# Where span attention's steps stand in the first stretch of a half batch: ahead of the second product with the values, or behind it

## The chip, the cores and the metric

The kernel runs on one core of a Trainium2 chip. The metric is the device time of one execution in microseconds (us), the median of three runs. All data are 32-bit floats. The engines of the core are PE (matrix products), DVE (vector operations), ACT (activations and copies), POOL (a second, slower engine for elementwise work) and SP (which issues transfers). Each runs its own instructions in order; they wait for each other by semaphores.

## What is computed

One layer of a perceiver: cross attention of 64 positions per batch element over a context of 1601 keys, then span attention over the 64 positions, then a feed-forward part with a shared expert and eight routed ones. Each part has a layer norm in front and a residual around it. There are 32 batch elements, a model width of 256 and 16 heads of 16.

```python
def reference(x, ctx_1024, mask_1x1xSxS2_bf1, ...):
    def _L0_xattn_ref(q, k, v, mask, ...):
        qh = _split_heads(q @ wq_w.T + wq_b)
        kh = _split_heads(k @ wk_w.T + wk_b)
        vh = _split_heads(v @ wv_w.T + wv_b)
        scores = jnp.einsum('bhqd,bhkd->bhqk', qh, kh) / jnp.sqrt(jnp.float32(D_K))
        scores = jnp.where(mask, scores, jnp.float32(-1000000000.0))
        attn = jax.nn.softmax(scores, axis=-1)
        out = jnp.einsum('bhqk,bhkd->bhqd', attn, vh)
        ...
        return out @ wo_w.T + wo_b
    def _L0_attn_ref(h, W_span, W_val, W_out):
        ...
        mean = jax.nn.sigmoid(span[..., 0]) * m
        soft = jax.nn.softplus(span[..., 1])
        diff = pos[None, None, :] - mean[..., None]
        scores = -soft[..., None] * (diff * diff)
        attn = jax.nn.softmax(scores, axis=-1)
        out = jnp.matmul(attn, value)
        ...
        return out @ W_out.T
    ...
    x = x + _L0_xattn_ref(_layernorm(x, axis=-1), ctx_1024, ctx_1024, mask_1x1xSxS2_bf1, ...)
    x = x + _L0_attn_ref(_layernorm(x, axis=-1), ...)
    x = x + _L0_ffn_ref(_layernorm(x, axis=-1), ...)
    return x
```

## The kernel before

**Tiling.** Cross attention goes by half batches: one batch element and 8 of its 16 heads. There are 64 of them, numbered n (b = n // 2, c = n % 2). The keys are cut into 13 blocks of 124, in four groups of 4, 3, 3 and 3 blocks. Scores are held transposed (keys on the partitions, four pairs of heads j = 0 to 3 beside each other). Two batch elements make a tile of 128 rows for the query projection, span attention and the feed-forward part: 16 tiles.

**The loop.** The main loop (L680) is a pipeline over half batches. In iteration n it computes the scores of half batch n + 1, the softmax of n, and the products of n - 1 with the values. It has four stretches, g = 0 to 3, one for each group of keys, which are counted through as 4n + g. PE, DVE, ACT and POOL execute their instructions in just the order in which the program issues them: the scheduler is held to it by `manual_schedule` (L648). So the order in the source is the order on each engine.

One iteration does this:

- Ahead of g = 0: `values(n-1, 0)` (L545), the first product with the values, 52 small products (104 matmul instructions, as each takes two) on PE, and the exponentials of the last pair of n - 1 on ACT.
- g = 0: `scores(n+1, 0)` (PE; DVE adds the mask to each of the four banks, L486), during which `turned_maxima(n)` transposes the maxima on PE (pm, L514) and DVE reduces them (mc, L521). Then one group of keys of the next batch element (pk, L442), and `maxima_along_rows` (L525), which spreads the maxima over the partitions on PE (pb, L529) and copies them on ACT (mb, L533). Then, for n above 0, `values(n-1, 1)`, the second product. If c = 0, that completes a batch element: `finish_steps(b-1)` (L620) is begun, its first piece copies the sums on ACT (o, L625), and the rest is put on the agenda of stretch 4n + 1 (L709). Then `less_maxima(n, 0)` (L536, POOL, 3.7 us each), `run(4n)`, and `first_maxima(n+1)` (L498), a copy on ACT with which the running maxima of the next half batch start.
- g = 1, 2, 3: `scores(n+1, g)` with the running maxima on DVE (L507) between the additions, keys (pk), values of the next batch element (pv, L458), `less_maxima(n, g)`, `run(4n+g)` and the exponentials of pair g - 1.

All of these products but the sums of the values and the running maxima take their PSUM bank from one pool of six.

**The agenda.** The short steps of the other parts are spread over the stretches. `agenda[s]` is a list of generators; `run(s)` (L614) takes the list in the order in which it was filled and advances each generator to its next `yield`, whose value says how many stretches later it goes on: it is then appended to that later stretch's list. Three kinds of generators use it:

- `span_steps(t)` (L214), 16 steps for a tile. It starts two stretches after the first of a half batch with n = 0 mod 4.
- `query_steps` (L402), the queries of the next tile, from the second stretch of n = 1 mod 4.
- `finish_steps` (L620): the sums' reciprocals (pr on PE, L628; rin on DVE, L632), and the product oT (DVE, L635), from which a tile's `span_steps` start one stretch later.

Since the period of a tile is four half batches, it is fixed what the first stretch of each holds:

| n mod 4 | steps in stretch 4n (`run(4n)`) |
|---|---|
| 0 | the span product po2 (16 products on PE, L327) and its copy o2T (ACT, L333) |
| 1 | two transposes tr_h (PE, L203) and the copy hT (ACT, L225) |
| 2 | the small operations on mean and slope (DVE, L273 to L289), which use part of the bank of the running maxima; the query product pq (PE, L412) and four copies qbd (ACT, L420) |
| 3 | one exponential (ACT, L305) |

In the stretch behind it, 4n + 1, stand for n = 0 mod 4 the rest of `finish_steps` and the span step po3 (PE, L337), x (DVE, L340), its statistics (DVE, L181 to L187), the power rstd_f (POOL, L189) and the transfer x_kept (SP, L342). For n = 2 mod 4 there are the rest of `finish_steps`, a span step on POOL (L294) and the last query step (POOL, L427).

The last half batch and the feed-forward part follow the loop and are not touched.

Of the kernel before, what the change touches and what calls it, by code (L numbers as in the profile page):

```python
# [76 lines left out]
def perceiver_kernel(ctx: ExitStack, tc: tile.TileContext, a: dict[str, bass.AP], out: bass.AP):  # L77
    nc = tc.nc
# [15 lines left out]
    def mm_bank(name: str):  # L94
        return ps_mm.tile([P, 512], F32, tag="mm", name=name)
# [277 lines left out]
    def pair_of(n: int, j: int):  # L373
        return prob[:CHUNK, place(n, j // 2), j % 2]
# [25 lines left out]
    def query_steps(t: int):  # L400
        spread = spread_of(xs[t], f"q{t}")
        yield 1  # L402
        xn = normalised(xs[t], spread, f"q{t}")
        yield 1
        ps = transposed(xn, f"q{t}")
        xnT = work.tile([P, 2, P], F32, tag="xnT", name=f"xnT_{t}")
        nc.vector.tensor_copy(xnT, ps)
        yield 1
        pq = mm_bank(f"pq_{t}")
        for c in range(2):  # L410
            for i in range(2):
                nc.tensor.matmul(  # L412
                    pq[:, c * P : (c + 1) * P], lhsT=wqT[:, i, c * P : (c + 1) * P],
                    rhs=xnT[:, i, :], start=(i == 0), stop=(i == 1),
                )

        q = work.tile([P, 2, 2, 2, S], F32, tag="qbd", name=f"qbd_{t}")
        for c in range(2):
            for e in range(2):
                nc.scalar.activation(  # L420
                    q[:, c, :, e, :], pq[:, c * P : (c + 1) * P].rearrange("p (b q) -> p b q", b=2),
                    AF.Identity, bias=bq4[:, c, e : e + 1], scale=own4[:, e : e + 1],
                )
        qbd[t] = q
        yield 1

        nc.gpsimd.tensor_tensor(xs[t], xs[t], bo_row, ALU.add)  # L427

    def load_context(b: int):
        for g in range(len(GROUPS)):  # L430
            load_piece(b, g)
        if b % 2 == 0 and b // 2 + 1 < NTILE:
            t = b // 2 + 1
            load_x(t)
# [34 lines left out]
    def scores(n: int, g: int, between=(), then=None):  # L469

        b, c = halves[n]
        c0, nb = GROUPS[g]
        pss = [mm_bank(f"psc_{b}_{c}_{g}_{j}") for j in range(4)]
        for k in range(nb):
            for j, ps in enumerate(pss):
                at = (c0 + k) * CHUNK
                nc.tensor.matmul(  # L477
                    ps[:CHUNK, k * P : (k + 1) * P],
                    lhsT=kTs[c][32 * j : 32 * j + 32, at : at + CHUNK],
                    rhs=qbd[b // 2][32 * j : 32 * j + 32, c, b % 2, :, :],  # L480
                    start=True, stop=True, tile_position=(32 * j, 0),
                )
        between = deque(between)
        held = then() if then else None
        for j, ps in enumerate(pss):
            nc.vector.tensor_tensor(  # L486
                pair_of(n, j)[:, c0 : c0 + nb, :].rearrange("p k (e q) -> p k e q", e=2),
                ps[:CHUNK, : nb * P].rearrange("p (k e q) -> p k e q", k=nb, e=2),
                madd[:CHUNK, c0 : c0 + nb, None, :].to_broadcast([CHUNK, nb, 2, S]), ALU.add,
            )  # L490
            if between:
                maximum(n, between.popleft())
            if j == 1 and held is not None:
                maxima_of_rows(*held)
# [3 lines left out]
    def first_maxima(n: int):  # L498
        nc.scalar.copy(mrun[:CHUNK].rearrange("p (r i) q -> p r i q", r=2), block_of(n, 0))  # L499

    def maximum(n: int, k: int):

        dst = mrun
        if k == NKC - 1:
            dst = mxs[n] = work.tile([P, 4, P], F32, tag="mx", bufs=1, name="mx")
        dst, run = (m[:CHUNK].rearrange("p (r i) q -> p r i q", r=2) for m in (dst, mrun))
        nc.vector.tensor_tensor(dst, block_of(n, k), run, ALU.max)  # L507

    def turned_maxima(n: int):

        m = mxs.pop(n)
        ps = mm_bank("pm")
        for j in range(4):
            nc.tensor.transpose(  # L514
                ps[:, j * CHUNK : (j + 1) * CHUNK], m[:CHUNK, j, :], ident[:CHUNK, :CHUNK]
            )
        return ps, work.tile([P, 4], F32, tag="mc", name="mc")
# [7 lines left out]
    def maxima_along_rows(col):  # L525

        ps = mm_bank("pb")
        for j in range(4):
            nc.tensor.transpose(  # L529
                ps[:CHUNK, j * P : (j + 1) * P], col[:, j : j + 1].to_broadcast([P, CHUNK]), ident  # L530
            )
        m = work.tile([P, 4, P], F32, tag="mb", bufs=1, name="mb")
        nc.scalar.copy(m[:CHUNK].rearrange("p j q -> p (j q)"), ps[:CHUNK])  # L533
        return m

    def less_maxima(n: int, j: int, m, engine):  # L536
        sj = pair_of(n, j)
        engine.tensor_tensor(  # L538
            sj, sj, m[:CHUNK, j, None, :].to_broadcast([CHUNK, NKC, P]), ALU.subtract
        )  # L540

    def exponentials(n: int, j: int):
        nc.scalar.activation(pair_of(n, j), pair_of(n, j), AF.Exp)  # L543

    def values(n: int, r: int):  # L545

        b, c = halves[n]
        v = vs[b % 2]
        for k in range(NKC):
            kn = min(CHUNK, KEYS - k * CHUNK)  # L550
            for j in range(4):
                h = 4 * r + j
                nc.tensor.matmul(  # L553
                    pvs[32 * j : 32 * j + DK + 1, c, r, :],
                    lhsT=v[:kn, k, 8 * c + h, :],
                    rhs=pair_of(n, h // 2)[:kn, k, (h % 2) * S : (h % 2) * S + S],
                    start=(k == 0), stop=(k == NKC - 1), tile_position=(0, 32 * j),
                )
# [29 lines left out]
    def linear_factor(u: int):  # L588
        quarter, hc = divmod(u, NHC)
        nc.scalar.activation(  # L590
            gated_at(quarter, hc), half_unit(u, sw3), AF.Identity, bias=b3twice[:, hc : hc + 1]
        )
        linear.add(u)
# [20 lines left out]
    def run(stretch: int):  # L614
        for steps in agenda.pop(stretch, []):
            wait = next(steps, None)
            if wait:
                agenda[stretch + wait].append(steps)
# [61 lines left out]
    for n, (b, c) in enumerate(halves[:-1]):  # L680
        if c == 0 and b + 1 < B:
            load_context(b + 1)
        if c and b % 2 == 0 and b // 2 + 1 < NTILE:
            agenda[4 * n + 1].append(query_steps(b // 2 + 1))

        def project(f, *args):
            if b + 1 < B:
                f(b + 1, *args)

        if n:  # L690
            values(n - 1, 0)
            exponentials(n - 1, 3)
        for g in range(len(GROUPS)):
            if g == 0:
                turned = []

                def turn():
                    turned.extend(turned_maxima(n))
                    return turned

                scores(n + 1, g, BETWEEN[g], turn)
                project(project_keys, c, 0)
                m = maxima_along_rows(turned[1])
                if n:
                    values(n - 1, 1)
                    if c == 0:
                        finish = finish_steps(b - 1, 4 * n + 1)
                        next(finish)
                        agenda[4 * n + 1].append(finish)  # L709
            else:  # L710
                scores(n + 1, g, BETWEEN[g])
                project(project_keys, c, g)
                if g == 1:
                    project(project_values, 3 * c)
                elif g == 2 and c:
                    project(project_values, 4)
                elif g == 3:
                    for u in range(5 if c else 1, 7 if c else 3):
                        project(project_values, u)
            less_maxima(n, g, m, nc.gpsimd)  # L720
            run(4 * n + g)
            for u in extra.get(4 * n + g, ()):
                linear_factor(u)
            if g == 0:
                first_maxima(n + 1)
            else:
                exponentials(n, g - 1)
        for k in BETWEEN[-1]:
            maximum(n + 1, k)
# [7 lines left out]
    m = maxima_along_rows(turned[1])  # L737
# [171 lines left out]
```

## Time and profile before

| | |
|---|---|
| median of 3 runs | 1637.11 us (1636.99 to 1639.4) |
| the profiled execution | 1636.38 us, its span 1634.6 us |
| granted clock of PE | 0.998 |
| four half batches (from one spreading of maxima to the fourth after it, 792.40 to 883.97) | 91.57 us |
| first product with the values to the scores behind it (n = 3 mod 4) | 1.58 us |
| POOL, one `less_maxima` | 3.73 us, 252 of them |

The profile is of one execution. Times count from the start of its span. A product's line in the timeline gives the start of its first matmul and the end of its last; since matmuls are pipelined, the distance between the starts of two groups tells how long the first holds the engine. PEld is the loading of the stationary operand, which overlaps the matmuls. A note in square brackets is the engine's idle time ahead of the instruction and what ended it. The chain of waits follows the work that ended last back in time, at each step to what released it, or to the instruction before it on its engine; an engine that is not on it has room.

### The profile page before, as it was taken

What the parts mean: (1) busy time and instruction counts of PE and PEld (TensorE: products, weight loads), DVE (VectorE), ACT (ScalarE), POOL (GpSimd) and SP (SyncE); (2) the same over time, 40 slices, a digit from 0 to 9 for tenths busy, and PEclk for the clock granted to TensorE, in tenths of its full rate; (3) what the DMA queues carried; (4) which work ended last, traced back from release to release, by engine and by line L of the source; (5) the groups of instructions that cost most, each with busy time, mean ns of one, the idle gap of its engine ahead of it and who ended that gap; (6) DMA issues with size and microseconds to landing.
All of it is one profiled execution on the core that took longest, in us unless ns stands there. A gap on an engine that the chain in (4) does not pass through costs nothing.

```text
span 1634.6 us, 55734 instructions
## 1 busy us (share of the span) xinstructions
PE 1568.6 (96%) x25128; PEld 1181.3 (72%) x25128; DVE 1290.9 (79%) x2636; ACT 910.2 (56%) x1261; POOL 1119.9 (69%) x424
## 2 busy tenths in 40 slices
PE   8999999999999999999999999999999999998999
PEld 5777777777777777777777777777777777765488
DVE  4888989888888979888888989888888989886300
ACT  3555556565565656565565556565665656555411
POOL 1777767767687768768687767767687767772620
PEclk9999999999999999999999999999999999999999
DMA  5111111111111111111111111111111111104100
GB/s 175 55 31 41 34 40 33 49 43 43 49 42 35 35 40 33 49 42 43 49 42 36 34 40 33 49 43 43 49 42 36 36 35 35 31 2 149 56 23 29
DMA packets 52045, 73.67 MB, mean 45 GB/s; under 512 B 3812, under 2 KB 51040, under 8 KB 51680
## 3 DMA queue, kind: packets, MB, share of 16 engines
q1 hardware_dynamic: 50992, 69.32, 14.7%
q8 instruction: 197, 3.23, 0.8%
q10 hardware_dynamic: 816, 0.79, 0.1%
q14 instruction: 40, 0.33, 0.1%
HBM read 65.90 MB, written 4.19 MB: 43 GB/s over the span
## 4 chain that ended last, share of the span: by engine, by line
PE 57%; DVE 39%; issue 2%; ACT 1%; POOL 0%; DMA 0%; ACTq 0%; DVEq 0%; POOLq 0%
DVE prob L486 13%; DVE mrun L507 13%; PE pk L442 13%; PE pv L458 13%; PE pvs L553 10%; PE psc L477 8%; PE py L838 3%; DVE rin L632 3%; PE pm L514 2%; PE u L582 2%; PE ph L820 2%; PE pb L529 1%; DVE least L302 1%; DVE mrun L287 1%; DVE total L307 1%
## 5 line engine op out<-in xcount | busy, mean ns | idle before, releaser
L538 POOL TENSOR_TENSOR prob<-prob,mb 124x1664 f32<-124x1664 f32 x252 | 935.4, 3730 | 326.6 <-ACT mb L533 319.8
L486 DVE TENSOR_TENSOR prob<-psc,madd 124x384 f32<-124x384 f32 (+1 forms) x1024 | 584.0, 583 | 179.4 <-PE psc L477 179.4
L507 DVE TENSOR_TENSOR mrun<-prob,mrun 124x512 f32<-124x512 f32 x704 | 483.6, 687 | 7.0 <-ACT mrun L499 4.0
L442 PE MATMUL pk<-ct,wkT_sb 128*128 128x372 f32 (+2 forms) x1024 | 408.3, 522 | 14.7 <-DMA wkT_sb<-in_wkT 5.8
L543 ACT ACTIVATE prob<-prob 124x1664 f32<-124x1664 f32 x256 | 400.0, 1587 | 4.9 <-DVE prob L538 2.6
L458 PE MATMUL pv<-wvT_sb,ct 128*124 128x256 f32 (+1 forms) x1664 | 384.6, 379 | 0.0
L458 PEld LDWEIGHTS pv<-wvT_sb,ct 128*124 128x124 f32 (+1 forms) x1664 | 310.2, 186 | 76.9 <-DVE prob L486 2.4
L477 PE MATMUL psc<-qbd,kT 32*124 32x128 f32 x6656 | 293.9, 286 | 30.2 <-DVE prob L486 26.1
L446 ACT ACTIVATE kT<-pk,cols 128x372 f32<-128x372 f32 (+2 forms) x256 | 151.8, 593 | 293.3 <-PE pk L442 292.8
L477 PEld LDWEIGHTS psc<-qbd,kT 32*124 32x124 f32 x6656 | 232.2, 181 | 103.4 <-DVE prob L486 51.9
L442 PEld LDWEIGHTS pk<-ct,wkT_sb 128*128 128x128 f32 x1024 | 174.5, 190 | 119.1 <-issue 30.2
L464 ACT COPY v<-pv 124x512 f32<-124x512 f32 (+1 forms) x224 | 124.7, 557 | 219.4 <-PE pv L458 219.4
L553 PE MATMUL pvs<-prob,v 124*17 124x64 f32 x13312 | 212.3, 220 | 0.0
L553 PEld LDWEIGHTS pvs<-prob,v 124*17 124x17 f32 x13312 | 189.9, 98 | 26.9 <-issue 26.1
L840 DVE SCALAR_TENSOR_TENSOR ot<-py,prob 128x256 f32<-128x256 f32 x16 | 6.8, 425 | 76.9 <-PE py L838 66.1
L582 PE MATMUL u<-xfT,sw_sb 128*128 128x512 f32 x128 | 58.6, 608 | 0.5 <-DVE xfT L348 0.4
L632 DVE RECIPROCAL rin<-pr 128x256 f32<-128x256 f32 x32 | 56.0, 1749 | 0.3 <-PE pr L628 0.3
L529 PEld LDWEIGHTS pb<-cst,mc 128*124 128x124 f32 x256 | 29.8, 135 | 35.8 <-DVE mc L521 30.0
L514 PE MATMUL pm<-cst,mx 124*128 124x124 f32 x256 | 40.3, 280 | 8.5 <-DVE mx L507 7.5
L507 DVE TENSOR_TENSOR mx<-prob,mrun 124x512 f32<-124x512 f32 x64 | 43.9, 686 | 2.2
L827 ACT ACTIVATE hT<-ph,cols 128x256 f32<-128x256 f32 x32 | 13.4, 471 | 57.5 <-PE ph L820 57.5
L582 PEld LDWEIGHTS u<-xfT,sw_sb 128*128 128x128 f32 x128 | 24.2, 194 | 27.8 <-issue 24.8
(127 smaller groups left out, 1221.9 us busy)
## 6 DMA issues: line engine op xcount, KB each, us to landing
ct<-in_ctxT SPq DMA_DIRECT2D x64, 372.0 KB, 3.2
ct<-in_ctxT SPq DMA_DIRECT2D x32, 496.0 KB, 3.6
ct<-in_ctxT SPq DMA_DIRECT2D x32, 361.0 KB, 3.1
w<-in_w SPq DMA_DIRECT2D x16, 256.0 KB, 5.7
x<-in_x SPq DMA_DIRECT2D x16, 128.0 KB, 2.1
x_kept<-x SPq DMA_DIRECT2D x16, 128.0 KB, 1.7
prob<-x_kept SPq DMA_DIRECT2D x8, 256.0 KB, 5.4
out<-ot SPq DMA_DIRECT2D x16, 128.0 KB, 1.9
```

Source lines behind the costliest of these rows:

```text
L442: nc.tensor.matmul(ps[:, :kn], lhsT=wkT[:, i, c * P : (c + 1) * P], rhs=cts[b][g][:, i, :kn], start=(i == 0), stop=(i == 1),)
L446: nc.scalar.activation(kTs[c][:, k0 : k0 + kn], ps[:, :kn], AF.Identity, bias=cols[:, B_K + c : B_K + c + 1])
L458: nc.tensor.matmul(ps[:kn, n * D : (n + 1) * D], lhsT=cts[b][g][:, i, k0 : k0 + kn], rhs=wvT[:, i, :], start=(i == 0), stop=(i == 1),)
L464: nc.scalar.copy(vs[b % 2][:kn, 2 * u : 2 * u + n, :, :DK], ps[:kn, : n * D].rearrange("p (n h d) -> p n h d", n=n, d=DK),)
L477: nc.tensor.matmul(ps[:CHUNK, k * P : (k + 1) * P], lhsT=kTs[c][32 * j : 32 * j + 32, at : at + CHUNK], rhs=qbd[b // 2][32 * j : 32 * j + ...
L486: nc.vector.tensor_tensor(pair_of(n, j)[:, c0 : c0 + nb, :].rearrange("p k (e q) -> p k e q", e=2), ps[:CHUNK, : nb * P].rearrange("p (k e ...
L507: nc.vector.tensor_tensor(dst, block_of(n, k), run, ALU.max)
L538: engine.tensor_tensor(sj, sj, m[:CHUNK, j, None, :].to_broadcast([CHUNK, NKC, P]), ALU.subtract)
L543: nc.scalar.activation(pair_of(n, j), pair_of(n, j), AF.Exp)
L553: nc.tensor.matmul(pvs[32 * j : 32 * j + DK + 1, c, r, :], lhsT=v[:kn, k, 8 * c + h, :], rhs=pair_of(n, h // 2)[:kn, k, (h % 2) * S : (h % ...
L582: nc.tensor.matmul(ps, lhsT=w[:, c, hc * P : (hc + 1) * P], rhs=xfT[:, c, :, slot], start=(c == 0), stop=(c == 1),)
L632: nc.vector.reciprocal(rin, pr[:, : 4 * S])
```

## The change

In the first stretch (g = 0) `less_maxima(n, 0)` and `run(4n)` now stand directly behind `maxima_along_rows`, ahead of the second product with the values and of the beginning of `finish_steps`. In the other stretches they stay where they are. The extra pieces (`linear_factor`) and `first_maxima` stay behind the product.

```diff
                 scores(n + 1, g, BETWEEN[g], turn)
                 project(project_keys, c, 0)
                 m = maxima_along_rows(turned[1])
+                less_maxima(n, g, m, nc.gpsimd)
+
+                run(4 * n)
                 if n:
                     values(n - 1, 1)
                     if c == 0:
@@ -717,8 +720,9 @@
                 elif g == 3:
                     for u in range(5 if c else 1, 7 if c else 3):
                         project(project_values, u)
-            less_maxima(n, g, m, nc.gpsimd)
-            run(4 * n + g)
+            if g:
+                less_maxima(n, g, m, nc.gpsimd)
+                run(4 * n + g)
             for u in extra.get(4 * n + g, ()):
                 linear_factor(u)
             if g == 0:
```

The lines between the two pieces of the diff, which it leaves alone:

```python
                        finish = finish_steps(b - 1, 4 * n + 1)
                        next(finish)
                        agenda[4 * n + 1].append(finish)
```

## The prediction

> **What bounds the kernel now.** I read the page first: its busy shares and the chain that ended last.
>
> ```profile
> PE 1568.6 (96%) x25128; PEld 1181.3 (72%) x25128; DVE 1290.9 (79%) x2636; ACT 910.2 (56%) x1261; POOL 1119.9 (69%) x424
> ...
> PE 57%; DVE 39%; issue 2%; ACT 1%; POOL 0%; DMA 0%; ACTq 0%; DVEq 0%; POOLq 0%
> ```
>
> The chain is nearly all PE and DVE, taking turns; ACT, POOL and DMA are 1% together. An edit counts only if it shifts PE where PE leads or DVE where DVE leads. Second, the waits of all engines: DVE's one large wait is for PE's scores, its wait for ACT's first maxima is small.
>
> ```profile
> DVE prob L486 <- PE psc L477: 179.4, 132, 8.4
> ...
> DVE mrun L507 <- ACT mrun L499: 4.0, 15, 0.6
> ```
>
> Third, the chain in order of time over one period of four half batches (792.40 to 883.97, 91.6 us). I name half batches by n mod 4, since the steps repeat so. In every first stretch PE runs pb, second product (pvs), steps, next scores (psc). This is n = 1 mod 4 (steps: tr_h), with tr_f, which stands before another product, for comparison, and then n = 3 mod 4, which has no PE step:
>
> ```profile
> 787.34 0.22 PE tr_f L203 x2
> 787.56 1.58 PE pvs L553 x104
> ...
> 793.00 1.58 PE pvs L553 x104
> 794.58 0.37 PE tr_h L203 x2
> 794.95 0.86 PE psc L477 x24
> ...
> 838.67 1.58 PE pvs L553 x104
> 840.25 0.90 PE psc L477 x24
> ```
>
> Two transposes cost 0.22 in front of a product, 0.37 between product and scores. This is n = 0 mod 4, first stretch and then the second, and the timeline of the same place:
>
> ```profile
> 861.80 0.45 PE po L327 x32
> 862.25 0.90 PE psc L477 x24
> ...
> 866.42 0.46 DVE prob L486
> 866.88 1.67 DVE rin L632
> 868.58 0.42 DVE oT L635
> 869.00 0.34 DVE x L340
> ...
> 870.26 0.46 DVE prob L486
> ```
>
> ```profile
> 866.13 0.59 PE L628 MATMUL pr<-o,cst 128*128 128x256 f32 x2
> ...
> 866.56 1.03 PE L337 MATMUL po<-woutT_sb,o2T 128*128 128x256 f32 x4
> 866.79 1.75 DVE L632 RECIPROCAL rin<-pr 128x256 f32<-128x256 f32 x1
> ```
>
> The second stretch is DVE's, without a gap: the last addition, then finish_steps (rin, oT), then the span step (x and its statistics), then the next additions. pr, a short product, is ready exactly when DVE comes to rin.
>
> **What the Trainium skill says.** TensorEngine Tiling (Array Packing), section Key Properties: "Mode switching requires drain". The trace agrees: first start to first start, a product followed by scores takes 1.58, of which 104 matmuls at 0.014 are 1.44, so 0.14 is the switch; a transpose step of 2 x 0.11 takes 0.31 in front of a product (809.12 to 809.43), so 0.09 is the switch. TensorE: Matmul & The Clock Gate, section "Architectural detail: the array is 16x 32x32, not 1x 128x128", calls ACT and DVE strict FIFO: an instruction that waits holds those behind it. The trace agrees on ACT: in n = 2 the copy of first maxima could run from 84.1 (last addition over) and runs at 87.72, behind o and four query copies.
>
> **The change part by part.** All in us; the counts are of the loop.
>
> less_maxima goes ahead of the product in program order only. On POOL nothing stands between (no step of a first stretch uses POOL), and it already starts right after the mb copy (793.83, copy over 793.76). Cost 0. No moved step issues a DMA, so SP's queue is passed by nothing; the steps' DMA (x_kept) is in the second stretch.
>
> n = 3 mod 4: the one step is an ACT exponential; no ACT instruction of the product stands beside it. Cost 0.
>
> n = 1 mod 4, 15 times (tr_h). Now: pb to pvs 0.53, pvs 1.58, tr_h 0.37, sum 2.48. After: pb without its switch 0.44, tr_h with a switch as before any product 0.31, pvs straight to scores 1.58, sum 2.33. Gain 0.15. The input (xn_h, ACT, over at 788.98) is 4 us early. The chain stays on PE from here to the next half batch, so all counts: 15 x 0.15 = 2.2. Bounds 0.09 to 0.24 each (the switch at 0.15 or at nothing).
>
> n = 2 mod 4, 15 times (pq for the queries; span attention's small DVE operations). PE saves the same 0.15, but from the second tile on DVE is the later one: it has some 4 us of small operations up to 819.10 + 0.17, while psc is there at 818.4. Gain 0. ACT: the four qbd copies (1.5) go ahead of o, which then ends near 817.9; the first-maxima copy waits for DVE's soft (819.27) in any case. Gain 0. But n = 2 itself has no small operations. There the chain goes pq, qbd copies, first-maxima copy, DVE (88.36). After: pq starts at 83.47, qbd runs 84.67 to 86.18, o to 86.6, the copy to 87.1, and DVE's maximum comes 0.48 after an addition that starts at 87.03, at 87.51. Gain 0.85, once; 0.6 to 0.9.
>
> n = 0 mod 4, 14 times (po on PE, o2T on ACT). po and pvs are both column tiled: between them the trace has no gap (po is 2.00 - 0.53 = 1.47 after pvs starts, 104 x 0.014). After: 0.53 + 0.45 + 1.58 = 2.56, as now. Gain 0; unseen is the order po, then pvs, so down to -0.15. On ACT o and o2T (0.37 each) change places; the last of the two starts at 862.32 in either case, so the first-maxima copy still ends near 863.19, 0.4 before DVE needs it.
>
> The same moves run(4n) ahead of the line that appends finish to the second stretch's list. So that list is turned round: the span step first, then finish. For n = 2 mod 4 the step is POOL's alone and nothing meets. For n = 0 mod 4 PE now runs po3 (L337, four matmuls) and then pr (L628, two), and DVE runs x (L340) and its statistics before rin and oT. PE comes to this point at 866.13 as now, being busy with values before it. po3 lasts 1.03, and DVE follows a 256-column product by 0.04 (the tail: 1499.88 to 1499.92): x starts at 866.13 + 1.07 = 867.20, where rin started at 866.79. DVE stands 0.41. What follows sums to the same 3.39 in either order (0.45 + 0.46 + 0.21 + 0.08 + 0.06 + 1.79 + 0.34), so all later work of DVE is 0.41 late, and PE's keys of the fourth stretch (873.97), which wait for DVE's last addition, with it. rin no longer waits for anything: pr is ready by 867.6. oT comes 1.7 later and span_steps' first product with it (869.95 to near 870.9), so the scores behind it start near 872.7 in place of 871.77; they wait for a bank until 872.90 now, 873.3 then, so that is covered by 0.3. Loss 14 x 0.41 = 5.7; 0.3 to 0.5 each. I checked the distance pr to rin at all 14: 0.63 to 0.67.
>
> rstd_f on POOL comes earlier by near 1.7; POOL is not on the chain. Sum: -2.2 - 0.85 + 5.7 = +2.65. The profiled execution's 1636.38 (span 1634.6 and 1.8 around it) becomes 1639.0; the median of the runs shown, 1637.11, is 0.73 above it, and the sum applied there gives 1639.7.
>
> **The rivals.**
> Forecast, 1639.7: gains of 3.1 outweighed by the turned list. About 0.2% (3.3 us) is what a measurement of this kernel can tell from no change, so this reads as the same, leaning slower. Its own range is 1637.6 to 1641.6.
>
> Faster, 1634.0: the 0.41 is absorbed, because PE or DVE has room before keys of the fourth stretch, and the gains of 3.1 stand alone. For it: PE waits twice for banks there (0.8 and 0.3). Against: those waits are for DVE itself, and the chain of waits goes through DVE without a gap.
>
> Slower, 1641.8: po in front of pvs pays a drain (stationary operands of 32 and 17 columns), at the price of any other switch, 0.15; 14 x 0.15 = 2.1 on top of the forecast. Place: the first stretch of n = 0 mod 4, where PE leads. It decides from 0.05 each, which takes the total past 3.3. Against it: no gap in the order pvs, po. Losing the gain at tr_h would weigh as much.
>
> Banks dealt out otherwise, 1640.7: if keys of the third stretch get the bank of pr, held by rin until 870.2, PE loses its cover and the keys of the fourth come 0.07 later, 14 x 0.07 = 1.0. The trace cannot exclude it: keys wait for rin there now (868.60).
>
> **How the numbers follow.** Forecast 0.55, banks 0.05, slower 0.25, faster 0.15. Over 1640.4 lie most of the slower case and the upper third of the forecast: 0.38. Under 1633.8 lies about half of the faster case and what I may not see: 0.11. The rest, 0.51, is within 0.2%. The range 1634.6 to 1642.6 leaves out under a tenth at each end.
>
> **What would show it.** Right: the scores 0.15 sooner after pb for n = 1 mod 4; a new DVE wait at L340 for PE's po, 14 times 0.3 to 0.4; rin after x; the first-maxima wait of n = 2 (0.62) gone. Wrong: no wait at L340; po to pvs longer than 0.5; pvs to scores longer than 1.6; the period of four half batches not 0.26 longer than 91.57 (0.41 - 0.15).

## The result and the profile after

The changed kernel takes 1640.31 us (median of 10 runs, 1639.05 to 1642.89), the kernel before 1635.8 us in as many runs (1634.66 to 1639.4). The ratio is 1.0028, with a 95% interval of 1.0018 to 1.0038: 4.5 us slower, 2.9 to 6.2. The two profiled executions, 1639.05 and 1636.38, are 2.67 us apart.

The page of the changed kernel, its busy shares and the chain that ended last:

```profile
PE 1567.7 (96%) x25128; PEld 1178.9 (72%) x25128; DVE 1291.2 (79%) x2636; ACT 907.6 (55%) x1261; POOL 1120.6 (68%) x424
...
PE 60%; DVE 36%; issue 2%; ACT 1%; POOL 0%; DMA 0%; SPq 0%; ACTq 0%; DVEq 0%; POOLq 0%
```

The work is the same, to a few us on each engine; only waits have moved. The waits of DVE in the changed kernel (who waited for whom: sum, times, longest, in us):

```profile
DVE x L340 <- PE po L337: 6.9, 15, 1.2
...
DVE mrun L507 <- ACT mrun L499: 3.4, 14, 0.2
```

The same wait before:

```profile
DVE x L340 <- PE po L337: 0.9, 1, 0.9
```

That one stands in the tail, behind the loop; the other 14 waits are new. In the second line, the one long wait of 0.62 (n = 2) is gone. Next the chain of waits of the changed kernel (start, length, what), in the first stretch of n = 1 mod 4:

```profile
792.53 0.44 PE pb L529 x4
792.97 0.22 PE tr_h L203 x2
793.19 1.58 PE pvs L553 x104
794.77 0.86 PE psc L477 x24
```

From pb to the scores it is 2.24 in place of 2.38 (the chain before has pb as below, and its scores at 794.95).

```profile
792.57 0.44 PE pb L529 x4
```

And in n = 0 mod 4, first and second stretch:

```profile
860.03 0.58 PE po L327 x32
860.61 1.46 PE pvs L553 x104
...
866.10 0.88 PE po L337 x4
...
867.00 0.43 DVE x L340
...
868.35 1.68 DVE rin L632
870.05 0.42 DVE oT L635
870.48 0.46 DVE prob L486
```

po and product together take 2.04. Before, the product stood first, and with the 0.45 of po they took 2.03, so their order costs nothing:

```profile
860.22 1.58 PE pvs L553 x104
```

In the second stretch the chain now enters DVE through po3 on PE, where before it stayed on DVE.

To see all 60 half batches at once I took the distance from one spreading of the maxima (pb) to the next, by n mod 4. Their usual values:

| interval that starts at | before | changed | times |
|---|---|---|---|
| n = 0 mod 4 (from 8) | 24.34 | 24.75 | 14 |
| n = 1 mod 4 (from 5) | 21.87 | 21.72 | 15 |
| n = 2 mod 4 | 23.79 | 23.78 | 14 |
| n = 3 mod 4 | 21.55 | 21.54 | 15 |
| n = 2 alone | 23.05 | 22.13 | 1 |

14 x 0.41 - 15 x 0.15 - 0.92 = +2.6. That is the sum of the prediction, term for term. But a few intervals in each profile are 0.3 to 1.1 us longer than the usual value. In the kernel before these add up to 3.25 (n = 12, 16, 20, 24), in the changed one to 3.9 (n = 12, 16, 17, 20, 56, 60). The median says 4.5, not 2.6, so the experiments had two questions: whether the terms are what I took them for, and what the long intervals are.

### The profile page after: what moved, and what is told of

Its sections match the earlier page's. It is cut to its first block, busy times and chain, and to the rows that moved or that the text cites. A ratio compares the mean times of both kernels' runs of the same rounds, so it can differ in the third digit from the quotient of the medians.

```text
span 1637.3 us, 55778 instructions
## 1 busy us (share of the span) xinstructions
PE 1567.7 (96%) x25128; PEld 1178.9 (72%) x25128; DVE 1291.2 (79%) x2636; ACT 907.6 (55%) x1261; POOL 1120.6 (68%) x424
## 3 DMA queue, kind: packets, MB, share of 16 engines
q8 instruction: 197, 3.23, 0.8%
## 4 chain that ended last, share of the span: by engine, by line
PE 60%; DVE 36%; issue 2%; ACT 1%; POOL 0%; DMA 0%; SPq 0%; ACTq 0%; DVEq 0%; POOLq 0%
PE pv L458 14%; PE pk L442 14%; DVE mrun L507 12%; DVE prob L486 12%; PE pvs L553 9%; PE psc L477 8%; PE py L842 3%; DVE rin L632 3%; PE pm L514 2%; PE u L582 2%; PE ph L824 2%; PE pb L529 1%; DVE least L302 1%; DVE mrun L287 1%; DVE total L307 1%
## 5 line engine op out<-in xcount | busy, mean ns | idle before, releaser
L538 POOL TENSOR_TENSOR prob<-prob,mb 124x1664 f32<-124x1664 f32 x252 | 936.1, 3733 | 323.5 <-ACT mb L533 316.8
L499 ACT COPY mrun<-prob 124x512 f32<-124x512 f32 x64 | 38.4, 599 | 25.1 <-DVE soft L289 21.9
```

Of the source, the lines that this page charges most:

```text
L538: engine.tensor_tensor(sj, sj, m[:CHUNK, j, None, :].to_broadcast([CHUNK, NKC, P]), ALU.subtract)
```

## The experiments

Theory: the loss is the turned list of the second stretch of n = 0 mod 4 (0.41 each), the gain 0.15 each at n = 1 mod 4 (by the prediction, one switch of the array less) and n = 2. Rivals: the steps in front of the product cost something in themselves; the turned list costs more than 0.41; the surplus of the median is spread between executions. The edits of the list turned, the kernel before shifted and DVE crossed are shown against the kernel before, all others against the changed one.

**The list turned, nothing moved.** The finish is put on the list behind the steps; PE's order in the first stretch stays.

```diff
                         next(finish)
-                        agenda[4 * n + 1].append(finish)
...
             run(4 * n + g)
+            if g == 0 and n and c == 0:
+                agenda[4 * n + 1].append(finish)
```

> Only the list of the second stretch is turned round; no step moves ahead of the product. My sum: DVE waits 0.41 us at L340 in 14 half batches, so 5.7 us slower than before (about 1.0035), with L340 waiting for PE's po 14 times or more, and rin behind x. If the turned list costs more outside the profile than in it (the changed kernel was 4.5 us slower in the median where the two profiles differ by 2.7), this is 7 us or more slower. If the turned list is harmless, no change within 1 us.

Measured: 1642.67 us against 1636.29, ratio 1.0039 (1.0025 to 1.0053), 6.4 us slower. The usual interval of n = 0 mod 4 is 24.74, and all other usual ones are as before. The turned list alone makes the whole loss.

**The steps moved, the list kept.**

```diff
                 less_maxima(n, g, m, nc.gpsimd)
+                if n and c == 0:
+                    finish = finish_steps(b - 1, 4 * n + 1)
+                    agenda[4 * n + 1].append(finish)
                 run(4 * n)
                 if n:
                     values(n - 1, 1)
                     if c == 0:
-                        finish = finish_steps(b - 1, 4 * n + 1)
                         next(finish)
-                        agenda[4 * n + 1].append(finish)
```

> The change, but finish_steps is put on the list before the steps run, so the list keeps its order. My sum: the gains alone, 15 times 0.15 (tr_h) and 0.9 (n = 2), so 3.1 us faster than before (0.998), no wait at L340. If the steps in front of the product have a cost of their own, less than 2 us faster or none.

Measured: 1637.32 us, ratio 1.0010 (1.0000 to 1.0019). The usual intervals are those expected (24.34, 21.73, and 22.13 at n = 2), so the 3.1 us of gain are there, and still the kernel is not faster. In its profile the long intervals add up to 7.0, 3.75 more than before: the gain is given back there. Four of them are at n = 1 mod 4 (13, 17, 21, 61), where the kernel before has none.

**The same without po.**

```diff
-                run(4 * n)
+                if n % 4 in (1, 2):
+                    run(4 * n)
...
             if g:
                 less_maxima(n, g, m, nc.gpsimd)
+            if g or n % 4 in (0, 3):
                 run(4 * n + g)
```

> Steps move ahead of the product only for n = 1 and n = 2 mod 4; po (n = 0) stays behind it with its list as before. My sum: the same as with all steps moved and the list kept, 3.1 us faster than before, since po gains nothing. If po in front of the product is what costs (a switch of the array, or the supply of instructions), this is 2 us faster than the kernel with the list kept.

Measured: 1636.93 us, ratio 1.0005 (0.9997 to 1.0013). The 3.1 us do not show here either. Whether po stands in front or behind makes no difference in the usual interval (24.33 and 24.34). The long intervals at n = 17, 21 and 61 stay. So these do not need the moving of po. The runs below with tr_h left behind the product, n = 2 moved or not, have none of them: they come with the moving of tr_h.

**The changed kernel again.**

> The changed kernel again, beside the others. My sum: 2.6 us slower than before. If what the medians showed (4.5 us) is real and not spread between executions, again 4 us or more.

Measured: 1642.27 us, ratio 1.0036 (1.0023 to 1.0048). The surplus over 2.6 is real. In this profile the long intervals add up to 6.3, 3.0 above those of before: 2.6 + 3.0 = 5.6, where the medians differ by 6.0. The two profiles of this one kernel are 2.4 apart in their long intervals, so a single profile tells their sum to some us only.

**What a long interval is.** The chain of the kernel before at n = 16, and two lines of the transfers between 400 and 405 us (one digit for each 0.125 us, tenths of the engines' busy time; then packets and MB of the queue that brings instructions):

```profile
401.62 0.65 PE psc L477 x16
402.26 0.56 issue
402.82 0.39 PE psc L477 x4
```

```profile
DMA  0004000000000000000000000000000040010000
...
q8 instruction: 2, 0.03, 2.3%
```

PE stops within the scores (I call this a stall) and waits for nothing that the profile shows. A packet of instructions begins at 400.44, is over at 401.37, and PE goes on 1.45 later. I counted PE's instructions (matmuls, loads of weights, semaphore waits; the first is number 0) in order of start up to the one with which PE goes on:

```
kernel              n         instruction   mod 256   packet over before it (us)
before              16, 20, 24    12737, 15809, 18881   193   1.45, 1.28, 1.32
list kept           17, 20, 21    13505, 15809, 16577   193   1.29, 1.31, 1.56
```

The number modulo 256 is the same each time, and so it is at all 59 long intervals of the twelve profiles: PE goes on with an instruction that is number 193 modulo 256, 1.2 to 1.6 us after a packet is over. It lies mostly in the scores behind a product, at times in po, in the product itself or at the first keys. The profile's page has 197 such packets of 3.23 MB together, 16.4 KB each. The Trainium skill (Runtime: NRT & Kernel Launch, section "Instruction fetch mechanics") says that instructions are refilled in 16 KiB blocks of 256 and that the cost of crossing a boundary is "mostly hidden". The packets agree; that it is hidden holds for most of the crossings (the kernel before has 4 long intervals to 197 packets), and not for these. Here PE works through short instructions: 256 of them (208 of a product, 48 of the scores behind it) take 1.58 + 0.86 = 2.44 us. A period of four half batches has 12 x 256 + 20 PE instructions in the kernel before, so the boundary moves by 20 each time and meets these places only in some periods. That can be tested.

**The kernel before, shifted.** Ahead of PE's first product, which waits for its weights at that time, 32 products of zeros.

```diff
+    pad = const.tile([P, 32], F32, name="pad")
+    nc.gpsimd.memset(pad, 0.0)
...
+    for _ in range(32):
+        nc.tensor.matmul(mrun[:32, 0, :32], lhsT=pad, rhs=pad, start=True, stop=True)
     queries = query_steps(0)
```

> The kernel before with 32 small products of zeros ahead of PE's first product, which still waits for its weights then: about 128 more PE instructions at the start, nothing else. If the stalls of PE in the scores of n = 16, 20 and 24 come from the instruction stream's packets of 256, they move to n = 40, 44 and 48 (perhaps 36), since a packet's end moves by 20 instructions in four half batches; the time stays within 1 us of before. If they come from the time or from other transfers, they stay at n = 16 to 24.

Measured: 1635.6 us against 1637.4, ratio 0.9988 (0.9980 to 0.9996). The long intervals are at n = 40, 44 and 48, and at no other n. The chain of this kernel at n = 40 (its lines from the padding on are numbered two higher):

```profile
949.59 0.45 PE po L329 x32
950.04 0.85 PE psc L479 x20
950.89 0.96 issue
951.85 0.48 PE psc L479 x3
```

The instructions with which PE goes on are 31425, 34497 and 37569: again 193 modulo 256. The stalls follow the position in the instruction stream, not the time. That it came out 1.8 us faster I had not expected, and the loop does not explain it (4.0 us of long intervals, not fewer). Most of it goes with the granted clock, shown further down.

**All moved, list kept, shifted by 100.**

```diff
+    for _ in range(25):
+        nc.tensor.matmul(mrun[:32, 0, :32], lhsT=pad, rhs=pad, start=True, stop=True)
```

> All steps ahead of the product, list kept, and 25 such products ahead of everything (about 100 instructions). If packets of 256 set the stalls, those of n = 12, 16, 20, 56, 60 and of 17, 21, 61 go, and three come at n = 40, 44, 48 and one or two near n = 45 and 49: some 2 us less than with the list kept and no shift, so 1 to 3 us faster than before. If they do not, the same time as with the list kept (1 us slower than before).

Measured: 1639.54 us, ratio 1.0012 (1.0004 to 1.0020), 2.1 us slower where 1 to 3 faster were expected. The time is a miss, the places half of one: the stalls went from all the old places and came at n = 40, 44, 48, as expected, but those of n = 1 mod 4 are not one or two but four, at n = 5, 41, 45 and 49, and together 5.9 us. At n = 41:

```profile
972.53 0.22 PE tr_h L203 x2
972.75 1.58 PE pvs L555 x104
974.32 0.86 PE psc L479 x23
975.18 1.85 issue
977.03 0.26 PE psc L479
```

A single stall of 1.85, twelve times the 0.15 that tr_h saves. In the shifted kernel before, n = 41 passes the same boundary with no stall: there the packet begins 0.08 ahead of pb, here 2.68 behind it. The other three are alike: at n = 5, 45 and 49 the packet begins 2.13, 1.06 and 1.00 ahead of pb there, and 1.02, 1.04 and 0.89 behind it here.

**Only n = 2 moved.**

```diff
-                run(4 * n)
+                if n == 2:
+                    run(4 * n)
...
+            if g or n != 2:
                 run(4 * n + g)
```

> Only n = 2 has its steps ahead of the product; all else as before. My sum: the one gain of 0.85 to 0.9, so 0.9 us faster (0.9995), with the stalls of PE where they are before. A rival for which a moved step costs something in itself: no gain.

Measured: 1637.35 us, ratio 1.0001 (0.9992 to 1.0009). In the profile the interval of n = 2 is 22.13 in place of 23.05; in the median 0.05% cannot be told from nothing. By the medians inconclusive for the time; at equal clock (below) it is 0.8 us faster.

**DVE crossed against PE.** The kernel before; in the second stretch pr stays ahead of po3 on PE, but DVE takes x and its statistics ahead of rin.

```diff
+        if apart:
+            yield
         rin = work.tile([P, 4 * S], F32, tag="rin", name=f"rin_{b}")
...
-                        finish = finish_steps(b - 1, 4 * n + 1)
+                        finish = finish_steps(b - 1, 4 * n + 1, True)
                         next(finish)
-                        agenda[4 * n + 1].append(finish)
...
+            if g == 1 and n and c == 0:
+                next(finish)
             run(4 * n + g)
+            if g == 1 and n and c == 0:
+                next(finish, None)
```

> The kernel before, but in the second stretch of n = 0 mod 4 DVE takes the span step (x and statistics) ahead of rin, while PE still runs pr ahead of po3. If DVE pays exactly the length of what PE has queued ahead of its operand, x can start 866.56 + 1.03 + 0.04 = 867.63 in place of rin at 866.79: 0.84 us in 14 half batches, 11.8 us slower. If the turned list costs 0.41 for another reason (order on DVE alone), 5.7 us.

Measured: 1649.19 us, ratio 1.0072 (1.0057 to 1.0087), 11.8 us slower. The interval of n = 0 mod 4 is 25.17: 0.83 each. The chain:

```profile
872.46 0.43 PE pr L628 x2
872.90 0.88 PE po L337 x4
...
873.80 0.43 DVE x L340
```

DVE pays what PE has queued up to its operand: 0.83, where the expectation had 0.84 and a cost of DVE's order alone would have left 0.41.

**Two versions that were to beat both.** The first: only n = 2 moved, and 32 products of zeros ahead.

> A version meant to beat both: the kernel before with only n = 2 moved and 32 products of zeros ahead of everything. The sum of the two runs' steady parts: 0.9 us from n = 2 and up to 2 from the shift, so 1 to 3 us faster than before (0.998 to 0.9994), stalls at n = 40, 44, 48 and none for n = 1 mod 4. If the shift's gain was chance of that session, 0.9 us or nothing.

Measured: 1635.67 us against 1636.59, ratio 0.9994 (0.9985 to 1.0002). Stalls at n = 40, 44 and 48 alone, none at n = 1 mod 4. The lower bound of what I expected, and by the medians not clear of no change; the gain of the shift did not come again in full.

The second has in addition the steps of n = 1 mod 4 ahead of the keys:

```diff
                 scores(n + 1, g, BETWEEN[g], turn)
+                if n % 4 == 1:
+                    run(4 * n)
                 project(project_keys, c, 0)
...
+            if g or n % 4 != 1 and n != 2:
                 run(4 * n + g)
```

> The same, and for n = 1 mod 4 the steps stand still further ahead, in front of the keys (between pm and pk), so the switch of the array behind the product is saved as in the change: 15 times 0.15. If the stalls for n = 1 mod 4 come from the product running straight into the scores with no short step between, stalls of 0.5 to 1.9 us at n = 41, 45, 49 take the gain back: no faster than the one without it. If they came from steps standing just ahead of the product, none appear and it is 2.2 us faster.

Measured: 1637.1 us, ratio 1.0003 (0.9995 to 1.0011). Both expectations missed. There are no stalls at n = 1 mod 4, though the product runs straight into the scores; the packets at n = 5, 41, 45 and 49 begin 1.2 to 3.3 us ahead of pb. And there is no gain: the interval ahead of pb grew by 0.41, the one behind it shrank by 0.37.

```profile
786.76 0.22 PE tr_h L203 x2
786.99 1.86 PE pk L444 x4
788.85 0.44 PE pb L531 x4
```

tr_h takes its 0.22, but pk takes 1.86 where it takes 1.67 behind pm (792.53 - 790.87 in the changed kernel): the 0.19 of one load of its weights, which is the mean of that load, now stands open. That it is this load is read from the number alone.

**The granted clock where the loop ends.** Each run of the experiments comes with PE's mean granted clock. In all traces it is 1.00 through the loop up to 1473 us and falls only behind that, for some us at a time: from 1478 to 1500 us it is 0.86 in the kernel before and 0.82 in the one without po, which has 0.94 from 1500 to 1560 too, where the kernel before has 1.00. The part from the last pb to the end took 156.6 us in the one and 160.2 in the other. The 85 runs of the kernel before follow the clock: means of 1635.4, 1636.4, 1638.1, 1639.0 and 1639.6 us at 0.999, 0.998, 0.997, 0.996 and 0.995. So the medians also differ by how many runs had which clock: of the shifted kernel before, 12 of 13 had 0.998 or more, of the kernel before beside it 15 of 33. The third column is an estimate from these figures: each run less the mean of the kernel before at the same clock, averaged, with a 95% interval. The last is the loop in the profile, from pb of n = 2 to pb of n = 62. All are us above the kernel before.

| kernel | median | at equal clock | loop in one profile |
|---|---|---|---|
| list turned | 6.4 | 5.2 (4.5 to 5.9) | 4.9 |
| list kept | 1.0 | 0.8 (0.3 to 1.5) | 0.3 |
| without po | 0.6 | -0.9 (-1.4 to -0.3) | -1.9 |
| changed, again | 6.0 | 4.8 (4.1 to 5.5) | 5.4 |
| before, shifted | -1.8 | -0.6 (-0.9 to -0.2) | 0.5 |
| list kept, shifted | 2.1 | 1.6 (1.0 to 2.3) | 2.3 |
| only n = 2 | -0.1 | -0.8 (-1.3 to -0.4) | -1.6 |
| crossed | 11.8 | 11.2 (10.7 to 12.0) | 11.4 |
| only n = 2, shifted | -0.9 | -1.3 (-1.7 to -0.9) | -1.6 |
| ahead of keys | 0.5 | -0.1 (-0.5 to 0.4) | 0.2 |

By this estimate the gain of n = 2 does show in the time, two thirds of the shift's 1.8 us went with the clock (the other 0.6 stays open), and without po the kernel is 1.7 us faster than with the list kept. The profile without po has fewer long intervals (4.8 against 7.0), so po in front may bring some as well; with one profile of each, this is not shown.

All profiles beside each other, in us of long intervals:

| kernel | n = 0 mod 4 | n = 1 mod 4 |
|---|---|---|
| before | 3.3 | 0 |
| changed; again | 3.3; 4.5 | 0.7; 1.8 |
| list turned | 2.8 | 0 |
| list kept; without po | 4.3; 2.6 | 2.7; 2.2 |
| list kept, shifted | 3.1 | 5.9 |
| before, shifted | 4.0 | 0 |
| only n = 2; crossed | 3.0; 3.3 | 0 |
| only n = 2, shifted; ahead of keys | 2.8; 3.7 | 0 |

The five profiles (of four kernels) with tr_h between pb and the product all have stalls at n = 1 mod 4; the seven others have none.

## Why the prediction was right, and what it left out

- less_maxima and n = 3 mod 4 at nothing: right (21.55 and 21.54; POOL's waits for the mb copy are 316.8 in place of 319.8).
- n = 1 mod 4, 0.15: right, 0.15 in all usual intervals. That it is a switch of the array is not shown by a run of its own. What I left out is that PE can stop here for its instructions. That 208 + 48 of them stand in a row is not enough for it: they do so at n = 3 mod 4 and with the steps ahead of the keys, where no profile has a stall. With tr_h in between, the packet also begins later.
- n = 2, 0.85: 0.92. The chain there no longer passes the query copies:

```profile
84.14 1.58 PE pvs L553 x104
85.72 0.90 PE psc L477 x24
86.61 0.54 DVE prob L486
```

- n = 2 mod 4 otherwise at nothing: right (23.79 and 23.78), hidden by DVE's small operations as said.
- po ahead of the product at nothing: right (2.04 against 2.03), so the slower rival of a drain between po and product falls.
- The turned list, 0.41: right, 0.41. The run with the list turned alone shows the whole loss, the crossed run shows what DVE pays for. The later oT is seen (PE's loads of weights for po at L215 wait 20.2 for it in all, 0.4 before) and covered, as the sum had it. So the faster rival, that the 0.41 is absorbed, falls as well. So does the rival of the banks, which asked for 0.07 more: the interval grew by 0.41, and the keys of the third stretch now start at 868.19, ahead of rin (868.35).
- The sum, +2.65, against +2.6 in the usual intervals and +4.5 (2.9 to 6.2) in the medians. The term that was missing is PE's supply of instructions: between 0.7 and 3.0 us more stalls than before in the two profiles of the changed kernel. The range held because it was open on the slower side, for other reasons. And that 1640.31 lies so near the forecast of 1639.7 is luck: three runs gave the kernel before 1637.11, ten gave 1635.8, and these 1.3 us made up for most of the 1.9 that the forecast change of 2.65 was short of the measured 4.5.

Why the packet begins later when tr_h stands between pb and the product stays open. In that place tr_h has a separate wait on a semaphore ahead of it (47 such waits at L203 with the list kept, 32 before); but so it has ahead of the keys (47 too), where there is no stall.

## What to carry to other kernels

Where a list of steps is filled in program order, moving the call that fills it moves later stretches too: go through every list that the moved code appends to, before counting what the move itself does. An operand that waits is paid for by all that the producer has queued ahead of it, so put first on the one engine what is first on the other. And a gain of a tenth of a us on an engine that issues many short instructions can be lost to the supply of instructions; look for stops that wait for nothing shown, and count where in the stream they fall.

## What I had not expected of the hardware

PE stopped within dense runs of short matmuls, each time at an instruction whose number is 193 modulo 256, 1.2 to 1.6 us after a packet of 16.4 KB of instructions was over; the intervals with such a stop were 0.25 to 2.1 us longer. 128 instructions more at the start moved the stops from n = 16 to 24 to n = 40 to 48, as counted in advance.

A step of two transposes costs 0.22 in front of a product, 0.37 between product and scores, and 0.41 between two groups of plain products, where the next group took 0.19 longer, the length of one load of its weights.

PE's granted clock was 1.00 through 1.4 ms of the loop and fell only from its end on. The executions of one kernel differ with its mean: 1635.4 us at 0.999, 1639.6 at 0.995.
